# Setup of a cross-attention kernel: Wk loaded in its own row order and turned ahead of y, and four head sums of batch 14 moved to ScalarE and Pool

## The chip, the cores and the metric

The kernel runs on one core of a Trainium2 chip. The metric is device time in microseconds of one execution, as the median of repeated runs. Beside it one execution was profiled. Engines are called as the profile calls them: PE (TensorE matmul), PEld (its weight loads), DVE (VectorE), ACT (ScalarE), POOL (GpSimd) and SP (SyncE, which here only issues DMAs).

## What is computed

The reference is a cross-attention layer in float32 for 16 batches of 100 queries (640 wide), 718 context rows (384 wide) and 4 extra tokens, with 8 heads of 80:

```
query = x @ Wq;  keyt = enc @ Wk;  valt = enc @ Wv
hs = mha(query, keyt, valt)
ca_q1 = einsum('btc,th->bch', ca, Wq_ca)[:, indices, :]
ca_hs1 = mha(ca_q1, x, x)
ca_hs2 = mha(ca_hs1 @ Wq, ca @ Wk_ca, ca @ Wv_ca)
out = (hs + ca_hs2) @ Wout + b_out + x
```

`mha` is softmax attention over 8 heads. The first line of the second path is small, but its scores go over 100 rows of x per batch.

## The kernel before

**Stages.** A setup part (lines 265 to 1482) loads the weights and makes what all batches share; a loop over 16 batches (line 1494 on) follows, in which every batch makes its scores (`s_ps`, L800), the maximum over keys on DVE, exponentials on ACT, the values' product with the weights (`a_ps`, L1799), and meanwhile the keys (`k_ps`, L481) and values (`v_ps`, L450) of later work. The setup is ordered by a scheduler from the program's text and its data waits, except where a line is bound with `in_order` (kept in program order on its engine) or `tc.issue_after` (after a named instruction). In the batch loop the order on each engine is that of the text (`manual_schedule`).

**Keys by sums.** The products `enc @ Wk` and `enc @ Wv` are made by a scheme with fewer block products (`K_PLAN`, `V_PLAN`): a block product takes a "form", a sum of blocks of `enc`, and a form of the weight, a sum of blocks of Wk. `weight_sums` (L546) makes the weight's forms in place in `wk_sb`: 12 subtractions of 128x256 on DVE. `enc_sums` (L516) makes those of `enc` on POOL. `Keys.go` (L481 for the matmuls, L421 and L423 for their evacuation) takes the forms one after the other, into the PSUM tiles `k_psA` to `k_psE`.

**The weight Wk.** The host hands Wk transposed (`wkt`, 640 rows of heads by 384). The kernel needs it untransposed, with the heads' first 64 columns sorted in `wk_sb` and their last 16 in `wk4`. Before, `load_packed` (L317) does the sorting in the load: eight DMAs of 64 rows and one of the rest, into the room of `kT`. Five groups of three 128x128 transposes on PE (`w_ps`, L1415) follow, and one ACT copy (L1418) for each group.

**y.** `Second.products` (L970) makes `y_ps` = x times `m2`, where `m2` is masked on POOL (`keys`, L941) from `m_sb`; `m_sb` is copied on DVE (L1399) from `m_ps` (L1391), the product of the transposed Wq with the token keys. `take` (L983) copies the first-path numbers `g` out of `y_ps`, for seven heads and then for the eighth; `copy` (L987) takes the rest. `scores1` (L999, L1006) makes the first-path scores `e` on POOL from `g`; `softmax1` (L891 to L1025) takes their maximum off on DVE.

**Wq.** Five loads `wq_in` into `st` (L323) are spread by heads into `wq_sb` on DVE: three copies for each load (L1426 twice, L1432), before `weight_sums`. The queries (`q_ps`, L560) need them.

**PSUM.** Three pools of two buffers each: `ps2` (two banks each), `psk` and `ps1` (one bank each). A tile waits until the last reader of its buffer is done.

**SP's queue.** All its loads stand in one order; a load's semaphore is shared with the load eight places ahead, whose landing it waits for.

**Batch 14.** `read(g)` (L1747, L1759) divides four heads of `a_ps` by their sums and adds the second path's `hs2`: a reciprocal and four DVE instructions. In batch 15, `vv.go` and `top.go` say in which order value products and steps of the maximum stand.

Of the kernel before, what the change touches and what calls it, by code (L numbers as in the profile page):

```python
# [10 lines left out]
ALU = mybir.AluOpType  # L11
# [3 lines left out]
B, S, H = 16, 100, 640  # L15
NH, D = 8, 80
CAD, T = 384, 4
SK = 722 - T
P = 128
HC = H // P  # L20
CC = CAD // P
# [7 lines left out]
ROWS = NH * S  # L29
# [26 lines left out]
for h in range(NH):  # L56
    lo = h * D
    while lo < (h + 1) * D:
        c = lo // P
# [8 lines left out]
RG = 4  # L68


KH = [(0, 64), (64, KN)]


def load_packed(load, to, w):

    rows = w.rearrange("(h k) n -> h k n", h=NH)
    for h in range(NH):
        r, c = divmod(h, RG)
        load(out=to[64 * r : 64 * r + 64, c], in_=rows[h, :64])
    load(out=to[:, 4], in_=rows[:, 64:])  # L80

V_PLAN = [
# [45 lines left out]
def kernel(  # L143
# [18 lines left out]
    nc = tc.nc  # L162
# [14 lines left out]
    def pair(name):  # L177
        tile = ps2.tile([P, 2, 512], F32, tag="ps2", name=name)
        return tile
# [80 lines left out]
    def in_order(dma):  # L260
        tc.keep_in_program_order(dma)
# [5 lines left out]
    wk_sb = const.tile([P, NF, 2, P], F32, name="wk_sb")  # L267
    wk4 = const.tile([P, CC, P], F32, name="wk4")
# [44 lines left out]
    in_order(nc.sync.dma_start(out=xT, in_=xt[0:2].rearrange("b p c s -> p b c s")))  # L313
    ca_0 = small.tile([S, T, S], F32, tag="ca", name="ca_0")
    in_order(nc.sync.dma_start(out=ca_0, in_=cas[0].unsqueeze(0).to_broadcast([S, T, S])))
    load_packed(
        lambda **ends: in_order(nc.sync.dma_start(**ends)), wkt_sb[:, :, :CAD], wkt  # L317
    )
    halves = [t[:, u] for t in sts for u in range(2)]
    room = halves.pop()  # L320
    wq_in = [t[:, :H] for t in halves]
    for c in range(HC):
        in_order(nc.sync.dma_start(out=wq_in[c], in_=wq[c * P : (c + 1) * P]))  # L323
    in_order(nc.sync.dma_start(out=wvca_sb, in_=wvca.rearrange("(c p) n -> p c n", p=P)))
# [199 lines left out]
    def weight_sums(engine, w, late=None, there={}):  # L524


        at = lambda f: there.get(f, w[:, W_AT[f]])
        raw = lambda c, g: w[:, 2 * (c - 1) + g - 1]
        if w is wk4:
            at, raw = w4_form, w4  # L530
        for f, left, right in (
            (0, raw(1, 2), raw(1, 1)),
            (11, raw(2, 2), raw(3, 2)),
            (12, raw(3, 2), raw(3, 1)),
            (5, raw(2, 2), raw(1, 2)),
            (7, raw(3, 2), at(5)),
            (13, raw(3, 1), at(7)),
            (1, raw(2, 1), raw(3, 1)),
            (3, raw(1, 1), at(7)),
            (6, raw(2, 1), raw(1, 1)),  # L540
            (10, raw(3, 1), raw(2, 2)),
            (2, raw(1, 1), raw(2, 2)),
            (14, raw(2, 1), raw(2, 2)),
        ):
            if late is None or late == (f in (5, 7, 13, 3, 14)):
                made = engine.tensor_tensor(at(f), left, right, ALU.subtract)  # L546
        return made
# [401 lines left out]
    class Second:  # L949
# [35 lines left out]
        def copy(self):  # L985
            self.y = y_sbs[self.b % 2]
            nc.scalar.copy(self.y[:, :, :HT], self.y_v[:, :, T:])  # L987
            if self.b > 1:
                self.take(0, NH)
# [398 lines left out]
    for c in range(HC):  # L1388
        m_ps = psum(f"m_ps_{c}")
        for n, heads in enumerate(HEADS):  # L1390
            nc.tensor.matmul(  # L1391
                m_ps[:, heads[0] * B * T : (heads[-1] + 1) * B * T],
                wqt_sb[:, n, c * P : (c + 1) * P],
                k2T[n],
                start=(n == 0),
                stop=(n == HC - 1),
                skip_group_check=True,
            )
        copied = nc.vector.tensor_copy(  # L1399
            m_sb[c].rearrange("p (b h t) -> p h b t", h=NH, t=T),  # L1400
            m_ps.rearrange("p (h b t) -> p h b t", h=NH, b=B),
        )
        nc.sync.dma_start(out=m_d[c], in_=m_sb[c])
    second = Second(0, xT, ca_0)
    enc_sums(enc)
    masked = keys(load_m(0))
    second.products()
    summed = second.take(0, NH - 1)
    second.copy()

    order = (HC - 1, *range(HC - 1))
    for c in order:
        w_ps = psum(f"w_ps_{c}")
        for cc in range(CC):
            nc.tensor.transpose(  # L1415
                w_ps[:, cc * P : (cc + 1) * P], wkt_sb[:, c, cc * P : (cc + 1) * P], ident
            )
        act(  # L1418
            wk_sb[:, c % 2 : 6 : 2, c // 2] if c < HC - 1 else wk4,
            w_ps[:, : CC * P].rearrange("p (a n) -> p a n", a=CC),  # L1420
        )

    with tc.issue_after(summed.ins):
        for c in range(HC):
            for r in range(2):
                nc.vector.tensor_copy(  # L1426
                    wq_sb[:, c, : 4 * P].rearrange("p (n r k) -> p n r k", n=RG, r=2)[
                        :, :, r
                    ],
                    wq_in[c].rearrange("p (r n k) -> p r n k", r=2, n=RG)[:, r, :, :64],  # L1430
                )
            moved = nc.vector.tensor_copy(  # L1432
                wq_sb[:, c, 4 * P :].rearrange("p (h k) -> p h k", h=NH),
                wq_in[c].rearrange("p (h k) -> p h k", h=NH)[:, :, 64:],
            )
    with tc.issue_after(moved.ins):
        made = weight_sums(nc.vector, wk_sb)
    with tc.issue_after(made.ins):
        second.take(NH - 1, NH)
    made = second.scores1()  # L1440
    with tc.issue_after(made.ins):
        weight_sums(nc.gpsimd, wk4)
        nc.scalar.copy(
            sts[0].rearrange("p a r -> p (a r)")[96:],
            low[96:].to_broadcast([P - 96, 2 * ROWS]),
        )
    with tc.issue_after(masked.ins):
        keys(load_m(1))
    last_keys(0, enc)
    first_keys = Keys(0, enc)  # L1450
    first_keys.go(8)
    va = wide("va")[:, : H // 2]
    va_ps = bank("va_ps")
    turn[0] += 1
    for c in range(CC):
        for n in range(2):
            nc.tensor.matmul(
                va_ps[n * B * T : (n + 1) * B * T, : H // 2],
                cat_sb[:, c, :],
                wvca_sb[:, c, n * (H // 2) : (n + 1) * (H // 2)],  # L1460
                start=(c == 0),
                stop=(c == CC - 1),
            )
    nc.scalar.copy(va, va_ps[:, : H // 2])
    va_d = dram.tile([B * T, H], F32, name="va_d")
    for n in range(2):
# [2 lines left out]
            in_=va[n * B * T : (n + 1) * B * T],  # L1469
        )  # L1470
    first_keys.go(NF)
    with tc.issue_after(first_keys.added.ins):
        second.softmax1()

# [18 lines left out]
    for b in range(B):  # L1493
# [59 lines left out]
            kk = Keys(b + 1, enc)  # L1553

        if b == 0:
            second.scores1()
            m_next = load_m(b + 2)
            kk.go(3)
            top.go(3)
# [115 lines left out]
        else:  # L1675
# [67 lines left out]
        def read(g):  # L1743

            a_v = a_vs[g]
            rs = small.tile([S, 4], F32, tag="rs", name=f"rs_{b}_{g}")
            nc.vector.reciprocal(rs.unsqueeze(2), a_v[:, :, D : D + 1])  # L1747
            cols = slice(4 * g * D, 4 * (g + 1) * D)
            if b == 0:
                nc.vector.tensor_tensor(  # L1750
                    hs[:S, cols].rearrange("p (h d) -> p h d", h=4),
                    a_v[:, :, :D],
                    rs.unsqueeze(2).to_broadcast([S, 4, D]),
                    ALU.mult,
                )
# [12 lines left out]
        if b in MIXED:  # L1768
            steps = (0, 6), (0, 18), (1, 6)
# [112 lines left out]
```

## Time and profile before

| | |
|---|---|
| median of 3 runs | 909.16 us (908.6 to 909.4) |
| the profiled execution's own time | 908.96 us |
| its span, first to last instruction | 907.2 us |
| PE busy | 900.4 us, 12200 matmul instructions |
| DVE, POOL, ACT busy | 719.7, 705.8, 460.1 us |
| granted TensorE clock | 1.000 |

A row of a timeline gives the start, the length, the engine and line, the operation, out<-in and shapes, a count, and in brackets how long the engine was idle before and what ended that. Rows of matmuls are merged and overlap, since a matmul's record runs on while the next has begun; the step from one row's start to the next row's start is what the engine spent.

### The profile page before, as it was taken

The numbers are of one execution on the slowest core, as the hardware profiler recorded it, in microseconds if no ns is written. First come the engines' busy times: TensorE is split into PE (matmuls) and PEld (weight loads), VectorE is DVE, ScalarE is ACT, GpSimd is POOL, SyncE is SP. The second block draws the span as 40 slices with busy tenths as digits, with TensorE's granted clock in tenths as the row PEclk, the third lists the DMA queues.
The fourth block names the chain that finished last, engine by engine and source line by source line (L and its number), as shares of the span: only waits on it lengthen the run. The fifth ranks groups of instructions, "written<-read, shape, count | busy, mean of one in ns | idle before, by whom it ended". The sixth has DMA issues, their size and how long they took to land.

```text
span 907.2 us, 28486 instructions
## 1 busy us (share of the span) xinstructions
PE 900.4 (99%) x12200; PEld 747.1 (82%) x12200; DVE 719.7 (79%) x1285; ACT 460.1 (51%) x906; POOL 705.8 (78%) x683
## 2 busy tenths in 40 slices
PE   9999999999999999999999999999999999999998
PEld 6798889787797878878798787988879788797866
DVE  3569796989849898796987969888984899849983
ACT  2345543747437573644737446374742747436441
POOL 7687999797868879696896959958797688967623
PEclk9999999999999999999999999999999999999999
DMA  8731103031301312130121301103130031300211
GB/s 265 262 120 57 48 14 87 24 107 53 112 4 44 88 33 74 54 105 32 48 60 54 106 33 53 56 25 106 54 83 32 24 107 53 98 32 25 60 44 40
DMA packets 50730, 62.99 MB, mean 69 GB/s; under 512 B 13698, under 2 KB 37954, under 8 KB 50604
## 3 DMA queue, kind: packets, MB, share of 16 engines
q1 hardware_dynamic: 48956, 59.18, 21.4%
q8 instruction: 96, 1.57, 0.7%
q10 hardware_dynamic: 1024, 1.15, 0.4%
q0 software_dynamic: 624, 0.85, 0.3%
q14 instruction: 30, 0.25, 0.1%
HBM read 55.59 MB, written 5.57 MB: 67 GB/s over the span
## 4 chain that ended last, share of the span: by engine, by line
PE 92%; DVE 4%; DMA 2%; SPq 1%; issue 0%; ACTq 0%; DVEq 0%
PE a_ps L1799 12%; PE s_ps L800 11%; PE v_psA L450 10%; PE k_psA L481 9%; PE v_psB L450 8%; PE k_psB L481 7%; PE o_ps L1278 5%; PE k_psA L761 4%; PE v_psC L450 3%; PE k_psC L481 3%; PE q_ps L618 2%; PE q_ps L560 2%; PE v_psD L450 2%; PE v_psE L450 2%; PE q_psA L618 1%; DMA xT<-in_xt 1%
## 5 line engine op out<-in xcount | busy, mean ns | idle before, releaser
L999 POOL TENSOR_TENSOR e<-ca,g 100x800 f32<-100x800 f32 x64 | 100.7, 1584 | 98.6 <-ACT kT L423 78.7
L1799 PEld LDWEIGHTS a_ps<-vs,st 120*64 120x64 f32 (+3 forms) x3072 | 119.0, 124 | 10.1 <-issue 0.7
L1799 PE MATMUL a_ps<-vs,st 120*64 120x81 f32 (+3 forms) x3072 | 122.8, 233 | 0.0
L516 POOL TENSOR_TENSOR enc<-enc 128x240 f32<-128x240 f32 x144 | 109.1, 768 | 11.3 <-DMA enc<-in_enct 4.2
L1515 DVE TENSOR_TENSOR st<-st,over 120x1600 f32<-120x1600 f32 x48 | 115.1, 2400 | 0.0
L450 PE MATMUL v_psA<-wv_sb,enc 128*120 128x320 f32 x352 | 109.3, 433 | 0.0
L1110 POOL TENSOR_TENSOR hs<-vb,p 100x640 f32<-100x640 f32 x64 | 93.1, 1466 | 9.6 <-issue 4.8
L1117 POOL TENSOR_TENSOR hs<-hs,hs 100x640 f32<-100x640 f32 x48 | 93.2, 1942 | 3.8
L481 PE MATMUL k_psA<-enc,wk_sb 128*128 128x240 f32 x384 | 95.4, 371 | 0.6 <-DVE wk_sb L546 0.6
L1006 POOL TENSOR_TENSOR e<-e,e 100x800 f32<-100x800 f32 x48 | 91.9, 1914 | 3.8
L450 PE MATMUL v_psB<-wv_sb,enc 128*120 128x320 f32 x296 | 91.9, 433 | 0.0
L1523 ACT ACTIVATE st<-st 120x1600 f32<-120x1600 f32 x48 | 73.9, 1539 | 25.1 <-DVE st L1515 24.7
L481 PEld LDWEIGHTS k_psA<-enc,wk_sb 128*128 128x128 f32 x384 | 71.4, 190 | 17.1 <-DVE wk_sb L546 1.0
L450 PEld LDWEIGHTS v_psA<-wv_sb,enc 128*120 128x120 f32 x352 | 64.2, 183 | 25.0 <-DVE vs L421 0.5
L1527 DVE TENSOR_TENSOR most<-most,st 120x800 f32<-120x800 f32 x64 | 67.0, 1047 | 13.8 <-ACT st L850 12.3
L481 PE MATMUL k_psB<-enc,wk_sb 128*128 128x240 f32 x320 | 77.9, 366 | 0.0
L800 PE MATMUL s_ps<-qp,kT 64*56 64x100 f32 (+1 forms) x3072 | 73.7, 248 | 0.3 <-issue 0.3
L800 PEld LDWEIGHTS s_ps<-qp,kT 64*56 64x56 f32 (+1 forms) x3072 | 67.2, 130 | 5.9 <-issue 4.6
L450 PEld LDWEIGHTS v_psB<-wv_sb,enc 128*120 128x120 f32 x296 | 54.1, 183 | 21.9 <-DVE vs L421 0.4
L856 ACT COPY st<-s_ps 120x800 f32<-120x800 f32 x64 | 49.8, 830 | 39.6 <-PE s_ps L800 39.4
L1185 ACT COPY hsT<-turned_hs 32x160 f32<-32x160 f32 (+7 forms) x244 | 67.7, 278 | 3.0
L481 PEld LDWEIGHTS k_psB<-enc,wk_sb 128*128 128x128 f32 x320 | 60.7, 190 | 8.1
(209 smaller groups left out, 1898.3 us busy)
## 6 DMA issues: line engine op xcount, KB each, us to landing
vb<-va_d SPq DMA_DIRECT2D x62, 250.0 KB
enc<-in_enct SPq DMA_DIRECT2D x30, 240.0 KB
enc<-in_enct SPq DMA_DIRECT2D x15, 360.0 KB
xT<-in_xt SPq DMA_DIRECT2D x8, 500.0 KB
rest<-in_enct SPq DMA_DIRECT2D x31, 120.0 KB
xn<-in_x SPq DMA_DIRECT2D x11, 320.0 KB
out<-xn SPq DMA_DIRECT2D x11, 320.0 KB
ca<-in_cas SPq DMA_DIRECT2D x16, 156.2 KB
```

What stands on the lines that cost most here:

```text
L450: nc.tensor.matmul(at[0][j][:KN, : H // 2], a_form(self.enc, f)[:, j * KN : (j + 1) * KN], wv_there.get(f, wv_sb[:, W_AT[f]]), start=first ...
L481: nc.tensor.matmul(at[:, i * KT : (i + 1) * KT], wk_sb[:, W_AT[f], i], a_form(self.enc, f), start=(first and i == 0), stop=last, skip_grou ...
L516: nc.gpsimd.tensor_tensor(out, left, right, op)
L800: nc.tensor.matmul(s_ps[at][k0:k1, cols], w, rhs, start=not begun & {(at, k) for k in range(k0, k1, 32)}, stop=last, skip_group_check=True,)
L999: first = nc.gpsimd.tensor_tensor(to, self.ca[:, t, :].unsqueeze(1).to_broadcast([S, NH, S]), g[:, :, t].unsqueeze(2).to_broadcast([S, NH, ...
L1006: made = nc.gpsimd.tensor_tensor(e, e, to, ALU.add)
L1110: first = nc.gpsimd.tensor_tensor(to, self.vb[t][:S].rearrange("p (h d) -> p h d", h=NH), p2[:, :, t].unsqueeze(2).to_broadcast([S, NH, D] ...
L1117: nc.gpsimd.tensor_tensor(sums, sums, to, ALU.add)
L1185: nc.scalar.copy(self.hsT(r)[32 * m : 32 * m + 32, :, first - lo : end - lo], turned[32 * i : 32 * i + 32, :, m, first - at : end - at],)
L1515: return nc.vector.tensor_tensor(st[i], st[i], top.over[:KN].unsqueeze(1).to_broadcast([KN, 2, ROWS]), ALU.subtract,)
L1523: nc.scalar.activation(st[i], st[i], AF.Exp, scale=SCALE)
L1799: nc.tensor.matmul(a_v[lo:hi, h % 4], st[i // 2][: KEYS[i], i % 2, h * S + lo : h * S + hi], block(i, h // 4)[: KEYS[i], h % 4], start=(i ...
```

## The change

1. **Load of Wk.** Nine sorted loads become two in the weight's own row order (row blocks 0 and 1, then 2 to 4), and they stand ahead of the loads of x (`xT`) and of the tokens (`ca`), no longer behind them.
2. **Transposes.** `turn_wk(cc)` turns one of three column blocks in five transposes into a two-bank tile of `ps2`. The heads are sorted by its copies: ACT takes `wk4` (128 elements) and one half of `wk_sb` (256), DVE the other half (256). Blocks 0 and 1 stand ahead of y, block 2 behind it.
3. **Wq.** `weight_sums` comes first; then DVE spreads three of the five loads, and ACT the other two, behind the first eight steps of the keys.
4. **Smaller moves.** The fill of 32 rows of `sts[0]` (`st<-low`, ACT) stands behind the first keys. In batch 0 the first-path scores of batch 1 wait for the running maximum (`seen`). The first matmul for `va` is kept in program order.
5. **Batches 14 and 15.** The four products of the first half of batch 14 go to ACT, and one POOL addition of 100x320 adds `hs2`. In batch 15 the third of the value steps comes ahead of the last step of the maximum.

```
-    load_packed(
-        lambda **ends: in_order(nc.sync.dma_start(**ends)), wkt_sb[:, :, :CAD], wkt
-    )
+    for c0, c1 in ((0, 2), (2, HC)):
+        in_order(
+            nc.sync.dma_start(
+                out=wkt_sb[:, c0:c1, :CAD],
+                in_=wkt[c0 * P : c1 * P].rearrange("(c p) n -> p c n", p=P),
+            )
+        )
+    in_order(nc.sync.dma_start(out=xT, in_=xt[0:2].rearrange("b p c s -> p b c s")))
+    in_order(nc.sync.dma_start(out=ca_0, in_=cas[0].unsqueeze(0).to_broadcast([S, T, S])))
...
+    def turn_wk(cc):
+        w_ps = pair(f"w_ps_{cc}").rearrange("p a n -> p (a n)")
+        for c in range(HC):
+            made = nc.tensor.transpose(
+                w_ps[:, c * P : (c + 1) * P], wkt_sb[:, c, cc * P : (cc + 1) * P], ident
+            )
+            if c == 0:
+                in_order(made)
+        act(
+            wk4[:, cc].rearrange("p (h k) -> p h k", h=NH),
+            w_ps[:, :H].rearrange("p (h k) -> p h k", h=NH)[:, :, 64:],
+        )
+        for g, copy in enumerate((act, dve)):
+            copy(
+                wk_sb[:, 2 * cc + g].rearrange("p i (r k) -> p i r k", r=2),
+                w_ps[:, :H].rearrange("p (r i g k) -> p g i r k", r=2, i=2, g=2)[
+                    :, g, :, :, :64
+                ],
+            )
...
+    turn_wk(0)
+    turn_wk(1)
     second = Second(0, xT, ca_0)
     enc_sums(enc)
     masked = keys(load_m(0))
     second.products()
-    summed = second.take(0, NH - 1)
+    second.take(0, NH - 1)
     second.copy()
...
+    turn_wk(2)
+    made = weight_sums(nc.vector, wk_sb)
...
+    with tc.issue_after(made.ins):
+        moved = spread_wq(dve, range(3))
     with tc.issue_after(moved.ins):
-        made = weight_sums(nc.vector, wk_sb)
-    with tc.issue_after(made.ins):
         second.take(NH - 1, NH)
     made = second.scores1()
...
     first_keys.go(8)
+    spread_wq(lambda *ends: tc.keep_in_program_order(act(*ends)), range(3, HC))
...
-            second.scores1()
+            second.scores1(seen)
...
+            vv.go(3)
+            top.go()
             vv.go(2)
-            top.go()
-            vv.go(3)
...
+                if b == B - 2 and g == 0:
+                    nc.scalar.mul(hs[:S, part], a_v[:, h, :D], rs[:, h : h + 1])
+                    continue
...
+            if b == B - 2 and g == 0:
+                nc.gpsimd.tensor_tensor(hs[:S, cols], hs[:S, cols], hs2[:, cols], ALU.add)
```

**PE, from y to the first keys.** In these rows `y_ps` is y, `w_ps` a group of transposes (its input `kT` is the room that Wk was loaded into), `kT_ps` the keys of the last 128 columns, which need `wk4`. Before:

```order
L970 MATMUL y_ps_358<-m_142,xT_121 36x108
L1415 MATMUL w_ps_372<-ident,kT 128x128 x3
L970 MATMUL y_ps_358<-m_142,xT_121 64x72
L970 MATMUL y_ps_358<-m_142,xT_121 36x72
L1415 MATMUL w_ps_377<-ident,kT 128x128 x3
L1415 MATMUL w_ps_387<-ident,kT 128x128
L1415 MATMUL w_ps_382<-ident,kT 128x128 x3
L1415 MATMUL w_ps_387<-ident,kT 128x128 x2
L702 MATMUL kT_ps_453<-enc_97,wk_88 128x240
L1415 MATMUL w_ps_392<-ident,kT 128x128 x3
L702 MATMUL kT_ps_453<-enc_97,wk_88 128x240 x2
```

Of the change, from the end of y (its last two rows) to the second pass over `k_psA`; the ten transposes of blocks 0 and 1 stand ahead of all ten rows of y:

```order
L951 MATMUL y_ps_369<-m_135,xT_121 64x72
L951 MATMUL y_ps_369<-m_135,xT_121 36x72
L1389 MATMUL w_ps_383<-ident,kT 128x128 x5
L683 MATMUL kT_ps_441<-enc_97,wk_88 128x240 x3
L683 MATMUL kT_ps_441<-rest_98,wk_88 128x240
L683 MATMUL kT_ps_441<-enc_97,wk_88 128x240 x4
L683 MATMUL kT_ps_441<-rest_98,wk_88 128x240
L462 MATMUL k_psA_453<-enc_97,wk_sb 128x240 x2
L462 MATMUL k_psB_457<-enc_97,wk_sb 128x240 x2
L462 MATMUL k_psD_461<-enc_97,wk_sb 128x240 x2
L462 MATMUL k_psA_453<-enc_97,wk_sb 128x240 x2
```

The transposes moved from behind y to ahead of it, all but five, and `k_psD`, which stood ahead of the first `k_psA`, now stands behind `k_psB`.

**DVE, the same stretch.** `wq_sb<-st` is the spread of Wq, `wk_sb<-wk_sb` the subtractions, `g` the copy out of y whose last piece POOL waits for. Before:

```order
L1426 COPY wq_sb<-st_82 128x4x64 x2
L1432 COPY wq_sb<-st_82 128x128
L1426 COPY wq_sb<-st_83 128x4x64 x2
L1432 COPY wq_sb<-st_83 128x128
L546 TENSOR_TENSOR wk_sb<-wk_sb 128x256 x12
L983 COPY g_369<-y_ps_358 100x4
L421 TENSOR_TENSOR kT<-k_psA_465,kT 128x2x240
```

Of the change:

```order
L1399 COPY wk_sb<-w_ps_342 128x256
L964 COPY g_380<-y_ps_369 100x28
L527 TENSOR_TENSOR wk_sb<-wk_sb 128x256 x3
L1399 COPY wk_sb<-w_ps_383 128x256
L527 TENSOR_TENSOR wk_sb<-wk_sb 128x256 x8
L1421 COPY wq_sb<-st_81 128x4x64 x2
L1427 COPY wq_sb<-st_81 128x128
L1421 COPY wq_sb<-st_81 128x4x64 x2
L1427 COPY wq_sb<-st_81 128x128
L1421 COPY wq_sb<-st_82 128x4x64 x2
L1427 COPY wq_sb<-st_82 128x128
L964 COPY g_380<-y_ps_369 100x4
```

The subtractions came ahead of the spread, four of them ahead of the last block's copy; the first `k_psA` product needs the fifth subtraction behind that copy (form 7, in place 5 of `wk_sb`). A copy of DVE out of a `w_ps` waits until ACT's two copies out of it are done.

**SP, the loads behind the first context rows.** Before:

```order
L287 DMA enc_97<-in_enct 128x240 x3
L313 DMA xT_121<-in_xt 128x2x500
L315 DMA ca_123<-in_cas 100x400
L317 DMA kT<-in_wkt 64x384 x8
L317 DMA kT<-in_wkt 128x1x384
L323 DMA st_81<-in_wq 128x640 x2
```

Of the change:

```order
L264 DMA enc_97<-in_enct 128x240 x3
L296 DMA kT<-in_wkt 128x2x384
L296 DMA kT<-in_wkt 128x3x384
L301 DMA xT_121<-in_xt 128x2x500
L302 DMA ca_122<-in_cas 100x400
L304 DMA st_81<-in_wq 128x640 x2
```

Seven loads are gone, and Wk stands where x stood.

More of the change, by code (lines that the diff above doesn't have):

```diff
@@ L71 @@
 KH = [(0, 64), (64, KN)]
[L74 to L80, printed above, removed]
 V_PLAN = [
@@ L312 @@
     xT = inp.tile([P, 2, HC, S], F32, tag="xT", name="xT_0")
-    in_order(nc.sync.dma_start(out=xT, in_=xt[0:2].rearrange("b p c s -> p b c s")))
     ca_0 = small.tile([S, T, S], F32, tag="ca", name="ca_0")
-    in_order(nc.sync.dma_start(out=ca_0, in_=cas[0].unsqueeze(0).to_broadcast([S, T, S])))
-    load_packed(
-        lambda **ends: in_order(nc.sync.dma_start(**ends)), wkt_sb[:, :, :CAD], wkt
-    )
     halves = [t[:, u] for t in sts for u in range(2)]
@@ L1407, with spread_wq @@
     second.products()
-    summed = second.take(0, NH - 1)
+    second.take(0, NH - 1)
     second.copy()
[L1411 to L1424, printed above, removed]
+    turn_wk(2)
+    made = weight_sums(nc.vector, wk_sb)
+    def spread_wq(copy, chunks):
+        for c in chunks:
             for r in range(2):
-                nc.vector.tensor_copy(
+                copy(
                     wq_sb[:, c, : 4 * P].rearrange("p (n r k) -> p n r k", n=RG, r=2)[
@@ L1431 @@
                 )
-            moved = nc.vector.tensor_copy(
+            moved = copy(
                 wq_sb[:, c, 4 * P :].rearrange("p (h k) -> p h k", h=NH),
@@ L1435 @@
             )
+        return moved
+    with tc.issue_after(made.ins):
+        moved = spread_wq(dve, range(3))
     with tc.issue_after(moved.ins):
-        made = weight_sums(nc.vector, wk_sb)
-    with tc.issue_after(made.ins):
         second.take(NH - 1, NH)
@@ L1442 @@
         weight_sums(nc.gpsimd, wk4)
[L1443 to L1446, printed above, removed]
     with tc.issue_after(masked.ins):
@@ L1456 @@
         for n in range(2):
-            nc.tensor.matmul(
+            made = nc.tensor.matmul(
                 va_ps[n * B * T : (n + 1) * B * T, : H // 2],
@@ L1463 @@
             )
+            if c == n == 0:
+                in_order(made)
     nc.scalar.copy(va, va_ps[:, : H // 2])
@@ L1471 @@
     first_keys.go(NF)
+    in_order(
+        nc.scalar.copy(
+            sts[0].rearrange("p a r -> p (a r)")[96:],
+            low[96:].to_broadcast([P - 96, 2 * ROWS]),
+        )
+    )
     with tc.issue_after(first_keys.added.ins):
```

## The prediction

> **What bounds the kernel now.** I read the page first, then the waits of PE, then PE's windows and timeline where those waits lie, then the chain of waits there, and at last the other engines beside it. The page's first line, and the shares by engine of the chain that ended last:
>
> ```profile
> span 907.2 us, 28486 instructions
> PE 92%; DVE 4%; DMA 2%; SPq 1%; issue 0%; ACTq 0%; DVEq 0%
> ```
>
> The span is 907.2 us, and the end is set by PE. So an edit counts only if it takes away PE work or a wait of PE, or adds one. These are PE's three longest waits of the whole run (total, times, longest; none other is over 0.3):
>
> ```profile
> PE idle_ps L1352 <- DVE idle L1349: 1.1, 1, 1.1
> PE k_psA L481 <- DVE wk_sb L546: 0.6, 1, 0.6
> PE w_ps L1415 <- DMA kT<-in_wkt: 0.6, 1, 0.6
> ```
>
> Two of them, 0.6 us each, are what the setup part of the change touches: the first keys wait for a subtraction, and the transposes wait for the load of Wk. Windows of PE (length, then PE busy) tell how much is to be had there, and how little behind it:
>
> ```profile
> 27.30:36.28 8.98, 7.72 (x59) 1.00 1.00 341
> 49.87:907.30 857.43, 853.11 (x11876) 1.00 0.19 58
> ```
>
> From the start of y to the first `k_psA`, PE is idle for 1.26 us of 8.98; its pipeline hides some more. After 49.87 it is busy for 99.5%. The stretch itself, row by row:
>
> ```profile
> 27.31 0.83 PE L970 MATMUL y_ps<-m,xT 128*64 128x72 f32 x16
> 28.76 0.52 PE L1415 MATMUL w_ps<-ident,kT 128*128 128x128 f32 x3 [0.62 <-DMA kT<-in_wkt]
> ...
> 29.48 1.20 PE L1415 MATMUL w_ps<-ident,kT 128*128 128x128 f32 x9
> 30.52 0.57 PE L702 MATMUL kT_ps<-enc,wk 128*128 128x240 f32 x2
> ...
> 32.63 1.78 PE L702 MATMUL kT_ps<-enc,wk 128*128 128x240 f32 x8
> 34.26 0.57 PE L702 MATMUL kT_ps<-rest,wk 128*128 128x240 f32 x2
> 34.66 0.97 PE L481 MATMUL k_psD<-enc,wk_sb 128*128 128x240 f32 x4
> 36.28 1.08 PE L481 MATMUL k_psA<-enc,wk_sb 128*128 128x240 f32 x4 [0.64 <-DVE wk_sb L546]
> ```
>
> What ended last before that last row is in the chain (the start, the length, the piece):
>
> ```profile
> 26.98 5.91 DMA st<-in_wq
> ...
> 33.54 2.69 DVE wk_sb L546 x8
> ```
>
> The fifth load of Wq lands at 32.89, DVE spreads it, and only then subtracts; the eighth subtraction, 2.69 us on, frees `k_psA` at 36.23.
>
> **The gain, if nothing new waits.** Step costs come from dense runs: nine transposes from 29.48 to 30.52, 0.116 us each; eight `kT_ps` products from 32.63 to 34.26, 0.204 each. For y I take these two rows of batch 0:
>
> ```profile
> 65.97 0.96 PE L970 MATMUL y_ps<-m,xT 128*64 128x72 f32 x20
> 66.86 1.08 PE L481 MATMUL k_psA<-enc,wk_sb 128*128 128x240 f32 x4
> ```
>
> They give 0.89 us for all of y. The same work packed from 27.31: 15 transposes 1.73, y 0.89, 18 products `kT_ps` 3.67, together 6.29, so `k_psA` could start at 33.60 where it started at 36.28. That is 2.68 earlier, but the first `k_psD`, 0.81 by the four products of the chain's next row, went ahead of it and now stands behind. **Bound of the gain: 1.87 us.**
>
> ```profile
> 37.35 0.81 PE k_psB L481 x4
> ```
>
> **Loads.** Transposes now stand first at 27.31, so Wk must have landed. SP before:
>
> ```profile
> 10.91 0.52 SPq L313 DMA_DIRECT2D xT<-in_xt  x1
> 11.98 13.04 SPq L317 DMA_DIRECT2D kT<-in_wkt  x9
> ```
>
> By the chain, the load of x issued at 10.91 landed at 23.17. Wk's first load takes that slot and is smaller; I estimate both of Wk by 22 to 24. x and the tokens come behind with no wait of SP for lanes of seven more loads, x near 25 (needed at 28.5), Wq near 26 to 30, needed only behind the subtractions, near 34. All are covered; if Wk's cover of 3 us were gone, each us of it would be a us of PE.
>
> **DVE and ACT, the new chain.** Copies out of the transposes have these neighbours:
>
> ```profile
> 29.32 0.48 ACT L1418 COPY wk<-w_ps 128x384 f32<-128x384 f32 x1 [8.07 <-PE w_ps L1415]
> 29.83 0.37 ACT L987 COPY y_sb<-y_ps 100x256 f32<-100x256 f32 x1
> 27.42 0.69 DVE L1399 COPY m<-m_ps 128x512 f32<-128x512 f32 x1 [0.63 <-PE m_ps L1391]
> 29.60 0.19 DVE L983 COPY g<-y_ps 100x28 f32<-100x28 f32 x1 [1.30 <-PE y_ps L970]
> ```
>
> So ACT takes 0.27 for 128 elements (below 0.37 by the 0.1 that 384 adds over 256) and 0.37 for 256; DVE 0.43 for 256, halfway between its two rows. A subtraction is 0.34 (2.69 over 8). ACT began 0.56 after the first of three transposes; with five it begins at 28.10 and is done with block 0 at 28.74. DVE: its copy of block 0 to 29.21, one subtraction to 29.55, the copy of block 1 to 29.98, `g` to 30.15. PE: ten transposes to 28.47, y to 29.36, block 2 to 29.94; then the first `kT_ps` waits for DVE's copy of block 1, some 0.08. The third `kT_ps` product needs block 2 of `wk4`. ACT has `y_sb` ahead of that copy, and `y_sb` waits for `g`: 30.18 to 30.55, `wk4` to 30.82, where PE is ready at 30.43. **That is a new wait of about 0.4, 0.5 with the 0.08.** `k_psA` then comes at 34.1. Its form is the fifth subtraction behind DVE's copy of block 2: three subtractions to 31.16, the copy behind ACT's last one from 31.22 to 31.65, five subtractions to 33.33. 0.7 us is spare there.
>
> The subtractions get a new neighbour, POOL's masks for batch 1:
>
> ```profile
> 26.25 0.97 POOL L941 TENSOR_TENSOR m<-m,hmask 128x96 f32<-128x96 f32 x3
> 28.87 2.15 POOL L941 TENSOR_TENSOR m<-m,hmask 128x96 f32<-128x96 f32 x4
> 64.85 2.02 DVE L1527 TENSOR_TENSOR most<-most,st 120x800 f32<-120x800 f32 x2 [0.95 <-ACT st L850]
> 67.46 3.23 DVE L1527 TENSOR_TENSOR most<-most,st 120x800 f32<-120x800 f32 x2
> ```
>
> The masks took 0.32 each with DVE on PSUM and 0.54 beside its copies in SBUF; DVE's maximum took 1.01 an instruction alone and 1.61 beside `e` on POOL, which started 0.2 later. So either engine can hold up the other. One subtraction stands ahead of `g` and three behind. Held up for nothing at the least and 0.54 (one mask) at the most, the one ahead adds 0 to 0.54 to PE's wait; I take 0.1, nearer to nothing, since the masks start late in its span. The other three have 0.7 of cover. **Sum: 1.87 - 0.5 - 0.1 = about 1.3 us gained.**
>
> The Trainium skill, "SBUF — State Buffer", section "SBUF: two separate sides", speaks against putting subtractions there: it calls the port pair that VectorE shares with GpSimd an exclusive lock, held for a whole instruction, so that a VectorE operation with two SBUF inputs waits out a GpSimd operation that reads SBUF. By it all four would wait, and the sum would be the first rival's below. The 1.61 against 1.01 agrees with a hold-up, not with one for the whole of POOL's 2.16 us.
>
> **Edits taken at nothing.** Two Wq loads (six copies, at most 0.48 each like the 384-element row) on ACT, and the fill behind the first keys:
>
> ```profile
> 44.13 0.43 ACT L1464 COPY va<-va_ps 128x320 f32<-128x320 f32 x1 [5.37 <-PE va_ps L1457]
> 31.39 1.52 ACT L1443 COPY st<-low 32x1600 f32<-32x1600 f32 x1
> ```
>
> ACT idles 5.37 us there, more than the six copies' 2.9. The fill can hold the first copy of a query back by some 0.4, and PE needs that buffer only four chunks later. Without the cover it would cost up to 1.5. In batch 0 POOL's scores of batch 1 wait for the maximum:
>
> ```profile
> 67.68 4.41 POOL L999 TENSOR_TENSOR e<-ca,g 100x800 f32<-100x800 f32 x2 [3.54 <-ACT st L856]
> 88.92 1.00 DVE L891 STREAM_TRANSPOSE turned<-e 128x800 f32<-128x800 f32 x1
> ```
>
> They would start up to 3 us later. The seven `e` steps need some 13.5 us, to 81.2 before; DVE reads the sum at 88.92, so 7 us cover it. Batch 14:
>
> ```profile
> 856.01 0.35 ACT L753 COPY kT<-k_psA 64x240 f32<-64x240 f32 x1 [2.83 <-PE k_psC L761]
> 873.01 0.24 POOL L1081 TENSOR_TENSOR e<-s,mx 100x32 f32<-100x32 f32 x1 [18.28 <-DVE mx L1079]
> 862.81 0.57 PE L800 MATMUL s_ps<-qp,kT 64*64 64x100 f32 x16 [0.34 <-issue]
> ```
>
> ACT is idle for 2.83 us and POOL for 18.28 where they get work. PE's only gap nearby is 0.34 with no engine named, so DVE's four instructions fewer free nothing that PE waits for. ACT's four products may delay the copy at 856.01; PE has other work between.
>
> **The rivals.** (1) *DVE is held up through the masks.* All four subtractions wait for half to all of a 0.54 mask. The one ahead of `g` puts 0.27 to 0.54 on PE's wait, the other three 0.8 to 1.6 against 0.7 of cover, so 0.1 to 0.9. The gain shrinks to 1.87 - 0.5 - 0.4 to 1.4, around 0.5: 908.4. For it: the two rows above. Against: the masks end near 31. (2) *The time saved is given back*: PE comes 1.3 us earlier to batch 0 and waits there for DVE or POOL, whose work didn't shrink: about 909.1. Against: PE's waits in the batches are a few tenths. (3) *The end gains too*: the 0.34 gap, 0.58 by steps, goes with other instruction streams: about 907.0. The row bears it out weakly, since no engine is named. (4) *Slower: PE stands behind Wk's load.* With transposes ahead of y nothing is left to fill the wait. If Wk lands later than 27.31, PE loses a us for each us; from 28.6 the gain is gone, from 30.4 the kernel is over 0.2% slower, and at 30.8, about 911. For it: the ninth load before landed only at 28.7. Against: that one was issued up to 14 us behind x.
>
> **How the numbers follow.** 0.2%, 1.82 us, is about what a measurement of this kernel can tell from no change; faster means below 907.34. Against the profiled execution's own 908.96, the forecast is 907.66; against the median of 909.16, 907.86. I say **907.7**, with its own range from 907.1 (no new wait) to 908.3. Chances: forecast 0.60; rival 1 0.14; rival 2 0.09; rival 3 0.11; rival 4 0.06. The range, 906.7 to 908.9, takes in rivals 1 and 3 and leaves out the other two. Faster: 0.20 of the forecast's 0.60 and 0.10 of rival 3, so 0.30; slower 0.06; the rest, 0.64, is the same.
>
> **What would show it.** Right: transposes from 27.3 without a wait for the load; `k_psA` near 34.1; a wait of PE at the third `kT_ps` for ACT; subtractions of 0.34 behind the masks. Wrong: a wait of PE for `in_wkt`; a `wk_sb` wait ahead of `k_psA`, with subtractions over 0.6; or `k_psA` early and a new wait in batch 0 or 1.

## The result, and the profile after

| | kernel before | changed kernel |
|---|---|---|
| median, 21 runs each on one chip | 908.36 us (906.73 to 909.72) | 906.35 us (905.47 to 907.87) |
| ratio, 95% interval | | 0.9979 (0.9973 to 0.9986) |
| the profiled execution's own time, its span | 908.96, 907.2 us | 907.72, 906.0 us |

The change makes the kernel 1.9 us faster (1.3 to 2.5, by the interval times 908.36). The forecast was a gain of 1.3 us, at the low edge of that, and a time of 907.7 in a range from 906.7: the measured 906.35 lies below the range. 0.8 us of the miss is the level of the kernel before, which was 909.16 in the three runs that the forecast started from and 908.36 in 21; the rest is a gain that was sized too small.

PE's waits of the whole run in the changed kernel (total, times, longest):

```profile
PE idle_ps L1333 <- DVE idle L1330: 1.1, 1, 1.1
PE k_psC L462 <- DVE vs L402: 0.3, 1, 0.3
PE k_psA L462 <- DVE kT L402: 0.2, 1, 0.2
```

Both waits of the setup that the forecast spoke of, 0.6 us for Wk's load and 0.6 for a subtraction, are gone. A new one stands in the list: 0.2 us at `k_psA` for DVE's sums of the keys. PE's timeline of the changed kernel, from the first transpose to the first query:

```profile
27.31 1.26 PE L1389 MATMUL w_ps<-ident,kT 128*128 128x128 f32 x10
28.50 0.96 PE L951 MATMUL y_ps<-m,xT 128*64 128x72 f32 x20
29.39 0.77 PE L1389 MATMUL w_ps<-ident,kT 128*128 128x128 f32 x5
29.99 1.40 PE L683 MATMUL kT_ps<-enc,wk 128*128 128x240 f32 x6
31.22 0.57 PE L683 MATMUL kT_ps<-rest,wk 128*128 128x240 f32 x2
31.63 1.78 PE L683 MATMUL kT_ps<-enc,wk 128*128 128x240 f32 x8
33.25 0.57 PE L683 MATMUL kT_ps<-rest,wk 128*128 128x240 f32 x2
33.65 0.97 PE L462 MATMUL k_psA<-enc,wk_sb 128*128 128x240 f32 x4
...
47.77 2.53 PE L541 MATMUL q_ps<-xT,wq_sb 128*128 128x200 f32 x14
```

No row carries a bracket: PE runs from 27.31 to 47.77 without a wait. `k_psA` starts at 33.65; packed without any wait, the forecast had it at 33.60. In the windows (length, PE busy) the stretch is full, where it held 1.26 us of idle time before:

```profile
27.30:33.65 6.35, 6.35 (x55) 1.00 0.96 358
33.65:47.77 14.12, 14.12 (x74) 1.00 0.47 139
47.77:906.00 858.23, 853.73 (x11876) 1.00 0.20 59
```

The **setup stretch**, from PE's first instruction at 27.31 to the first query, is 47.77 - 27.31 = 20.46 us. Before, the same stretch ended with this row, and was 49.87 - 27.31 = 22.56:

```profile
49.87 0.33 PE L560 MATMUL q_ps<-xT,wq_sb 128*128 128x200 f32 x1
```

So the setup gained 2.10 us, in one profile against one. The profiled executions differ by only 1.24; 0.6 of the rest is lost at one place in batch 1 (below), and some 0.2 stays open.

On DVE and ACT, the rows that the forecast's chain of copies was built on:

```profile
28.63 0.42 DVE L1399 COPY wk_sb<-w_ps 128x256 f32<-128x256 f32 x1 [0.23 <-ACT wk_sb L1399]
29.09 0.42 DVE L527 TENSOR_TENSOR wk_sb<-wk_sb 128x256 f32<-128x256 f32 x1
29.43 0.42 DVE L1399 COPY wk_sb<-w_ps 128x256 f32<-128x256 f32 x1
29.77 0.18 DVE L964 COPY g<-y_ps 100x28 f32<-100x28 f32 x1
29.88 1.34 DVE L527 TENSOR_TENSOR wk_sb<-wk_sb 128x256 f32<-128x256 f32 x3
31.15 0.41 DVE L1399 COPY wk_sb<-w_ps 128x256 f32<-128x256 f32 x1
31.48 2.76 DVE L527 TENSOR_TENSOR wk_sb<-wk_sb 128x256 f32<-128x256 f32 x8
```

```profile
29.98 0.37 ACT L968 COPY y_sb<-y_ps 100x256 f32<-100x256 f32 x1 [0.83 <-DVE g L964]
30.25 0.27 ACT L1394 COPY wk<-w_ps 128x128 f32<-128x128 f32 x1
30.40 0.39 ACT L1399 COPY wk_sb<-w_ps 128x256 f32<-128x256 f32 x1
```

`g` ended at 29.95 (forecast 30.15) and the last block of `wk4` at 30.52 (forecast 30.82). The three subtractions beside POOL's masks took 0.42 each from start to start (29.88 to 31.15), the eight behind them 0.34.

### The profile page after: what moved, and what is told of

It reads as the page before. It is cut to its first block, busy times and chain, and to the rows that moved or that the text cites. A ratio compares the mean times of both kernels' runs of the same rounds, so it can differ in the third digit from the quotient of the medians.

```text
span 906.0 us, 28486 instructions
## 1 busy us (share of the span) xinstructions
PE 900.3 (99%) x12200; PEld 748.1 (83%) x12200; DVE 720.6 (80%) x1278; ACT 461.9 (51%) x917; POOL 712.8 (79%) x684
## 4 chain that ended last, share of the span: by engine, by line
PE 94%; DVE 5%; ACT 0%; DMA 0%; issue 0%; DVEq 0%
PE a_ps L1806 12%; PE s_ps L781 12%; PE v_psA L431 10%; PE k_psA L462 8%; PE v_psB L431 8%; PE k_psB L462 6%; PE o_ps L1259 5%; PE k_psA L742 4%; PE v_psC L431 3%; PE k_psC L462 3%; PE v_ps L372 2%; PE q_ps L599 2%; PE q_ps L541 2%; PE v_psD L431 2%; PE v_psE L431 2%; PE k_psE L462 1%
## 5 line engine op out<-in xcount | busy, mean ns | idle before, releaser
L980 POOL TENSOR_TENSOR e<-ca,g 100x800 f32<-100x800 f32 x64 | 97.9, 1540 | 90.9 <-ACT kT L404 67.4
L497 POOL TENSOR_TENSOR enc<-enc 128x240 f32<-128x240 f32 x144 | 113.2, 796 | 14.2 <-DMA enc<-in_enct 7.2
L1091 POOL TENSOR_TENSOR hs<-vb,p 100x640 f32<-100x640 f32 x64 | 90.6, 1426 | 3.8 <-DMA vb<-va_d 1.5
```

Source lines behind the costliest of these rows:

```text
L497: nc.gpsimd.tensor_tensor(out, left, right, op)
L980: first = nc.gpsimd.tensor_tensor(to, self.ca[:, t, :].unsqueeze(1).to_broadcast([S, NH, S]), g[:, :, t].unsqueeze(2).to_broadcast([S, NH, ...
L1091: first = nc.gpsimd.tensor_tensor(to, self.vb[t][:S].rearrange("p (h d) -> p h d", h=NH), p2[:, :, t].unsqueeze(2).to_broadcast([S, NH, D] ...
```

## The experiments

Each kernel is the kernel before or the changed kernel with one edit. They ran in three groups, each on one chip with the kernel before beside it: the four of the first heading; the first three of the second with the first run of the kernel "kept apart"; and the others. The kernel before had 908.36, 908.14 and 908.41 us there. A ratio is to the kernel before of the same group; ratios and intervals stand as the measurement gave them, and differ by up to 0.0007 from the quotient of the two medians. Beside the time, the setup stretch is given, since it is free of what happens later.

### Each part alone

**Setup only.** The changed kernel with its edits to batches 14 and 15 taken back: `read(0)` of batch 14 on DVE again, and `vv.go(2)`, `top.go()`, `vv.go(3)` in the order of before.

> The change without its edits to batches 14 and 15. Theory (the setup carries the whole gain: PE's two waits around y and the keys): the time of the full change, 906.35 us, about 2.0 under the kernel before; in the profile k_psA starts at 33.65 as in the full change. Rival (the end gains too, since the gap of 0.5 us before the last scores is gone in the full change): 906.9, a gap of about 0.5 at that place.

906.86 us, ratio 0.9980 (0.9971 to 0.9989); stretch 20.46. The gap ahead of the last scores was not there either (in before, it was the row at 862.81 with 0.34 idle):

```profile
858.24 3.01 PE L781 MATMUL s_ps<-qp,kT 64*64 64x100 f32 x128
```

The setup carries most of the gain, and the gap doesn't belong to the edits of batch 14. The time alone doesn't settle it: 906.86 is the rival's figure, 0.9980 is nearly the ratio of the full change (0.9979), and the interval holds both 906.35 and 906.9.

**Batches 14 and 15 only**, the same edits made to the kernel before.

> The kernel before with only the edits to batches 14 and 15. Theory (PE waits for none of these instructions): no change, a ratio of 1.0000 within 0.0005. Rival (the end gains): 0.5 us faster, ratio 0.9994, and no gap before the last scores.

908.40 us, ratio 0.9993 (0.9983 to 1.0002): no difference from the kernel before, though the interval holds the rival's 0.5 us too. No row before the last scores shows idle time, as the rival said, but neither does one in the kernel with only Wk's loads moved (below), which lacks these edits. What tells more is that this kernel has the setup of before, instruction for instruction, and yet its profile differs there from the profile of before:

```profile
31.95 0.50 DVE L1426 COPY wq_sb<-st 128x256 f32<-128x256 f32 x2
32.37 0.22 DVE L1432 COPY wq_sb<-st 128x128 f32<-128x128 f32 x1
32.50 4.11 DVE L546 TENSOR_TENSOR wk_sb<-wk_sb 128x256 f32<-128x256 f32 x12
```

The spread of the fifth load of Wq began at 31.95 where it began at 32.91 in before, the subtractions with it, and the stretch was 48.89 - 27.18 = 21.71 instead of 22.56. PE's wait for Wk's load isn't in this profile at all. So **the old setup varies with its loads**, by 0.85 us in two draws, and against this draw the new setup gains only 21.71 - 20.46 = 1.25 us. The new one gave 20.45 or 20.46 in all seven profiles of kernels with its setup order (the others follow below).

**The subtractions ahead of the spread of Wq**, alone, in the kernel before:

```
     with tc.issue_after(summed.ins):
+        made = weight_sums(nc.vector, wk_sb)
+    with tc.issue_after(made.ins):
         for c in range(HC):
...
     with tc.issue_after(moved.ins):
-        made = weight_sums(nc.vector, wk_sb)
-    with tc.issue_after(made.ins):
         second.take(NH - 1, NH)
```

> The kernel before with one edit: the twelve subtractions stand ahead of the spread of Wq on DVE. Theory (the first keys waited for Wq's fifth load and its spread through DVE's order): the wait of 0.81 and the slow restart of 0.26 go, k_psA starts at 34.66 right behind kT_ps, the wait for Wk's load (0.87) stays: 1.1 us faster, ratio 0.9988. Rival (the last transposes' copies on ACT are the next to be late): k_psA at 35 or later, under 0.7 us gained.

```profile
27.74 0.83 PE L970 MATMUL y_ps<-m,xT 128*64 128x72 f32 x16
28.96 0.52 PE L1415 MATMUL w_ps<-ident,kT 128*128 128x128 f32 x3 [0.39 <-DMA kT<-in_wkt]
...
34.45 0.57 PE L702 MATMUL kT_ps<-rest,wk 128*128 128x240 f32 x2
34.85 0.97 PE L481 MATMUL k_psA<-enc,wk_sb 128*128 128x240 f32 x4
```

The mechanism is as expected: `k_psA` behind `kT_ps` without a wait, the wait for Wk still there, and the stretch 21.78, 0.78 under before. The time is not: 908.09 us, ratio 0.9997 (0.9988 to 1.0005), 0.3 us where 1.1 was expected. 0.3 of that went at 40, where the fill of `st`, now behind the keys' first copies on ACT, held one of them up, a sum on DVE waited for it, and PE for the sum; 0.7 went in batch 1 (2.63 us instead of 1.89 from `v_psA` to `k_psE`, as under "The loss in batch 1").

**Wk's nine loads ahead of those of x and the tokens**, alone, in the kernel before:

```
-    in_order(nc.sync.dma_start(out=xT, in_=xt[0:2].rearrange("b p c s -> p b c s")))
-    ca_0 = small.tile([S, T, S], F32, tag="ca", name="ca_0")
-    in_order(nc.sync.dma_start(out=ca_0, in_=cas[0].unsqueeze(0).to_broadcast([S, T, S])))
     load_packed(
         lambda **ends: in_order(nc.sync.dma_start(**ends)), wkt_sb[:, :, :CAD], wkt
     )
+    in_order(nc.sync.dma_start(out=xT, in_=xt[0:2].rearrange("b p c s -> p b c s")))
+    ca_0 = small.tile([S, T, S], F32, tag="ca", name="ca_0")
+    in_order(nc.sync.dma_start(out=ca_0, in_=cas[0].unsqueeze(0).to_broadcast([S, T, S])))
```

> The kernel before with one edit: Wk's nine loads stand ahead of those of x and the tokens. Theory (two waits in a row on PE, of which only the later one counts): the transposes no longer wait for their load, but the first keys still wait for Wq's fifth load and its spread, so k_psA stays near 36.3 and the time too, ratio 1.0000 within 0.0007; if x now lands behind 27.3, y waits, and that is hidden as well up to 1.8 us. Rival (each wait counts for itself): 0.9 us faster, ratio 0.9990.

```profile
PE k_psA L481 <- DVE wk_sb L546: 1.2, 1, 1.2
PE k_psD L481 <- DVE wk_sb L546: 0.2, 1, 0.2
```

The wait for Wk is gone from the list, and the wait for the subtraction has grown from 0.6 to 1.2: `k_psA` started at 36.40, where it was 36.28. Nothing was gained; 909.43 us, ratio 1.0015 (1.0002 to 1.0028). The two waits stood one behind the other, and only the later one counted. The stretch was 49.97 - 27.11 = 22.86. That the time came out slower was not expected: DVE waited 1.04 us for the fifth load of Wq, and the runs reached from 907.1 to 912.7:

```profile
33.03 0.50 DVE L1426 COPY wq_sb<-st 128x256 f32<-128x256 f32 x2 [1.04 <-DMA st<-in_wq]
```

### The changed kernel with one edit undone

**Three loads of Wq spread on DVE ahead of the subtractions** (`spread_wq(dve, range(3))` bound behind `take(0, NH - 1)`, `weight_sums` behind it).

> The change with one edit: DVE spreads its three loads of Wq ahead of the subtractions again (nine copies, about 1.6 us, behind the first copy out of y). Theory (place of the subtractions in DVE's order is half of the gain): the ninth subtraction, which the first k_psA product needs, ends near 35.0 where PE is ready at 33.65, so PE waits 1.3 and restarts slowly (0.26): 1.6 us slower than the change, 907.9, ratio to the kernel before 0.9996. Rival (the room in front of the keys is larger than read): 906.4, no wait at k_psA.

```profile
31.81 4.10 DVE L527 TENSOR_TENSOR wk_sb<-wk_sb 128x256 f32<-128x256 f32 x12
```

906.82 us, ratio 0.9983 (0.9974 to 0.9992), stretch 20.94. `k_psA` waited 0.24 and started at 33.95; the sixth of these twelve ends at 31.81 + 6 x 0.34 = 33.85. So here the first `k_psA` product needs the sixth subtraction, and not the ninth, on which the expected loss of 1.6 stood; the stretch lost 0.48. This doesn't carry over to the changed kernel, since the edit also changed the order of the subtractions. The product takes form 7 in both. `weight_sums` writes form 7 over a block of Wk that forms 11 and 12 still read, so it comes behind these two. In this kernel the scheduler issues the forms 0, 11, 12, 5, 1 and then 7, the sixth. In the changed kernel it issues 0, 5, 6 and 2 ahead of the last copy and 1, 11, 12, 10 and then 7 behind it, the ninth, as the section on the change has it. There form 7 is ready at 31.48 + 5 x 0.34 = 33.18, a little over 0.4 us before PE comes at 33.65.

**Wk's two loads behind x and the tokens.**

> The change with one edit: Wk's two loads stand behind those of x and the tokens. Theory (two loads instead of nine, not their place, take the wait away; Wk landed at 20.5 in the change and may land 2 us later): no wait at the transposes, 906.35, ratio 0.9979. Rival (the place matters, as the forecast took it): a wait of PE for in_wkt near 27.3 and up to 1 us more.

906.63 us, ratio 0.9983 (0.9974 to 0.9991), stretch 20.46, no wait for a load. Two loads in place of nine are enough; the place in the queue isn't needed. The 20.5 of the expectation is early for Wk as a whole: in the changed kernel SP waited 1.1 us for one of Wk's loads and issued the load of `wvca`, which stands eight places behind Wk's second one, at 22.16.

```profile
SPq L305 <- DMA kT<-in_wkt: 1.1, 1, 1.1
```

**All transposes behind y.**

> The change with one edit: all fifteen transposes stand behind y. Theory (the transposes ahead of y fill PE's wait for POOL's last masks, and start the chain of copies early): y waits about 0.6 for the mask that ends at 28.6, the copies out of the transposes come about 1.5 later, k_psA near 34.9 instead of 33.65: 1.3 us slower than the change, 907.6, ratio 0.9993. Rival (DVE and ACT have room): 906.4 to 906.9.

```profile
PE w_ps L1389 <- DVE wk_sb L1399: 0.5, 1, 0.5
PE y_ps L951 <- POOL m L922: 0.4, 1, 0.4
```

907.77 us, ratio 0.9999 (0.9990 to 1.0007); the stretch is 22.00, 1.5 longer than in the change. As expected, y waits for POOL's mask. The copies out of the transposes come later too, but PE meets them at the last five transposes and not at `k_psA`, where the expectation had it. So this order is worth most of the gain. The profile is of the slowest of the twelve runs (909.77), in which PE reached the stretch only at 29.00; the stretch is counted from there.

**`seen` taken out**: in batch 0, POOL's scores of batch 1 wait for nothing.

> The change with one edit undone: in batch 0 POOL's scores of batch 1 no longer wait for the running maximum. Theory (DVE's two steps of the maximum run beside POOL and take 1.6 instead of 1.0 us each, but PE has room there): within 0.2 us of the unedited change. Rival (the wait is part of the gain): 0.6 us or more above it, with a new wait of PE on DVE before 100 us.

906.76 us, ratio 0.9985 (0.9977 to 0.9994), stretch 20.45; the change unedited had 906.49 and 0.9982 (0.9973 to 0.9990) beside it (next heading). No difference that these runs can tell, and no new wait of PE on DVE before 100 us.

### The loss in batch 1

In batch 1 of the changed kernel, DVE and then POOL:

```profile
110.53 0.19 DVE L1060 TENSOR_REDUCE mx<-s 100x8 f32<-100x32 f32 x1
110.83 1.28 DVE L1062 TENSOR_TENSOR e<-s,mx 100x32 f32<-100x32 f32 x1
112.03 0.81 DVE L402 TENSOR_TENSOR vs<-v_psA,vs 120x640 f32<-120x640 f32 x1
```

```profile
110.52 3.03 POOL L980 TENSOR_TENSOR e<-ca,g 100x800 f32<-100x800 f32 x2
```

A subtraction of 100x32 took 1.28 us. POOL's first score had begun 0.31 before it and ended near 112.04 (half of 3.03), where DVE's ended at 112.11. In the kernel before, the same subtraction took 0.44, since POOL began its score only behind it:

```profile
112.85 0.44 DVE L1081 TENSOR_TENSOR e<-s,mx 100x32 f32<-100x32 f32 x1
113.97 3.03 POOL L999 TENSOR_TENSOR e<-ca,g 100x800 f32<-100x800 f32 x2
```

So it is in all fourteen profiles of this document: the subtraction took 1.26 to 1.29 us in the eight where POOL's score began before it, and 0.43 to 0.45 in the six where it began behind. When it is held up, DVE's sums of the keys come late, and PE waits. The Trainium skill, "SBUF — State Buffer", section "SBUF: two separate sides", calls the ports that VectorE shares with GpSimd an exclusive lock for a whole instruction, when a VectorE operation with two SBUF inputs meets a GpSimd operation that reads SBUF; the 1.28 us agree with it. The subtractions beside POOL's masks in the setup don't show it: they took 0.08 us more, where one of these masks took 0.32 in the kernel before with DVE on PSUM.

**The two kept apart**: in batch 1, POOL's first score waits for that subtraction instead of the running maximum.

```
-            second.scores1(seen, range(T - 1))
+            if b > 1:
+                second.scores1(seen, range(T - 1))
...
-            now.scores2(nc.vector if b == 1 else nc.gpsimd)
+            less = now.scores2(nc.vector if b == 1 else nc.gpsimd)
+            if b == 1:
+                second.scores1(less, range(T - 1))
```

> The change with one edit: in batch 1, POOL's first-path scores of batch 2 wait for DVE's small subtraction (e<-s,mx, 100x32) instead of for the running maximum. In the change's profile that subtraction took 1.28 us instead of 0.44, as long as POOL's first score was running beside it, and PE then lost 0.6 us at the keys at 114 to 116. Theory (DVE waits out POOL's instruction, and PE waits for DVE): the subtraction takes 0.44 again, PE loses nothing there, 0.5 us faster than the change, 905.8, ratio 0.9973. Rival (DVE is late there for another reason): the loss of 0.6 us stays, 906.4.

906.26 us, ratio 0.9977 (0.9969 to 0.9986). It ran a second time, beside the change unedited:

> The change itself, unedited, beside the next three on one chip. Theory: ratio to the kernel before 0.9979 as in its own runs, 906.4 us; in the profile the stretch from the first transpose to the first query is 20.46 us again, and the keys at 114 to 116 lose 0.6 again, if POOL's first score runs beside DVE's small subtraction.

> The change with the small subtraction of batch 1 kept apart from POOL's first score, as in e9_apart. Theory (the 0.6 us lost at the keys of batch 1 are kept): 0.4 to 0.6 us under the unedited change of the same call, near 905.9. Rival (given back later in the batches): within 0.2 us of the unedited change.

The change again: 906.49 us, ratio 0.9982 (0.9973 to 0.9990), stretch 20.46. Kept apart: 906.34 us, 0.9979 (0.9970 to 0.9988). PE at the keys of batch 1, first in the change again, then kept apart:

```profile
112.83 1.24 PE L431 MATMUL v_psA<-wv_sb,enc 128*120 128x320 f32 x4
114.27 1.05 PE L462 MATMUL k_psA<-enc,wk_sb 128*128 128x240 f32 x4 [0.20 <-DVE kT L402]
115.34 0.88 PE L462 MATMUL k_psE<-enc,wk_sb 128*128 128x240 f32 x3
```

```profile
113.22 1.24 PE L431 MATMUL v_psA<-wv_sb,enc 128*120 128x320 f32 x4
114.30 0.97 PE L462 MATMUL k_psA<-enc,wk_sb 128*128 128x240 f32 x4
115.11 0.97 PE L462 MATMUL k_psE<-enc,wk_sb 128*128 128x240 f32 x4
```

From `v_psA` to `k_psE` it is 2.51 us in the one and 1.89 in the other: the loss of 0.6 us is DVE's hold-up, and it goes when that goes (the subtraction took 0.44 again). In the time only 0.15 us of it can be seen, as the rival had it (within 0.2), and that is within the intervals. In these two profiles the 0.6 isn't given back: from the first query to the end it is 905.4 - 47.56 = 857.8 us in the change and 904.9 - 47.95 = 857.0 kept apart. But this part scatters too: 856.9 to 858.2 in the eight profiles with the hold-up, 856.3 to 857.4 in the six without. Why the medians show so little stays open. This version is the fastest of those that ran, but not by more than the measurement can tell.

### The third product of kT_ps

The changed kernel with the copy of `g` made twelve times, and the copies of y and of `wk4` bound behind it:

```
-    second.take(0, NH - 1)
-    second.copy()
-    turn_wk(2)
-    made = weight_sums(nc.vector, wk_sb)
+    for _ in range(12):
+        taken = second.take(0, NH - 1)
+        in_order(taken)
+    with tc.issue_after(taken.ins):
+        second.copy()
+        turn_wk(2)
+        made = weight_sums(nc.vector, wk_sb)
```

> The change with the copy of g out of y made twelve times on DVE (0.11 us each), and the copies of y and of the last block of wk4 bound behind it on ACT: it moves the copy that the third kT_ps product needs from 30.5 to about 31.4. Theory (each product is two records of 0.204, so the third starts at 30.8 and the copy was 0.3 early): PE waits 0.6 for ACT inside kT_ps. Rival (the forecast's reading, in which the third product was ready at 30.4): PE waits 1.0.

```profile
29.98 0.98 PE L683 MATMUL kT_ps<-enc,wk 128*128 128x240 f32 x4
32.81 0.67 PE L683 MATMUL kT_ps<-enc,wk 128*128 128x240 f32 x2 [1.85 <-ACT wk L1396]
```

907.85 us in one run. The twelve copies took 2.62 us, twice what I had reckoned, so the sizes of both expectations are off; the place is not. Four records run, and the fifth waits for ACT's copy of `wk4`. That copy ended at 32.75 here and at 30.52 in the change, 2.23 later; PE waited from 30.79, when it was ready, to 32.81, which is 2.02. The difference, 0.2 us, is the room that the change has at this place. There is no wait, but little more would make one.

## Why the forecast was right and wrong

- **What bounds the kernel** was right: two waits of PE in the setup, one behind the other. Alone, the load order gained nothing, and the subtractions first gained 0.78 us of stretch, of which 0.3 could be seen in the time; the order of the transposes, the loads and the subtractions together gave 2.10 us of stretch.
- **The bound of the gain, 1.87 us, was too small by 0.23.** Up to the first `k_psA` it held: 36.28 - 33.65 - 0.81 = 1.82 was gained, 0.05 less than packed. But behind that, to the first query, the old order took 49.87 - 36.28 = 13.59 and the new one 47.77 - 33.65 - 0.81 = 13.31 (`k_psD`, 0.81, stands there now). The 0.28 between them are three records of before that follow a wait and step by 0.31, 0.31 and 0.28 to the next, where others step by 0.20: at 36.28 behind DVE, and at 38.00 and 46.55 behind ACT's copies out of `k_psA`, for which the weight loads of these products waited:

```profile
38.00 0.70 PEld L481 LDWEIGHTS k_psA<-enc,wk_sb 128*128 128x128 f32 x4 [0.21 <-ACT kT L423]
46.52 0.50 PEld L481 LDWEIGHTS k_psA<-enc,wk_sb 128*128 128x128 f32 x3 [0.18 <-ACT kT L423]
```

In the change `k_psD` stands between the two passes, and none of the three is slow. So 1.82 + 0.28 = 2.10, by the profile of before from which the forecast was made.
- **The step that failed: the new wait of 0.5 us at the third `kT_ps` product.** I took 0.204 us as the time of a product and put the third one at 30.43. A product of this kind shows as two records in the profile: the order lists nine products where the timeline counts 18 records, and both stood in front of me. The third product starts with the fifth record, at 30.8. The right count alone, in the forecast's own sum, gives 29.94 + 0.08 + 4 x 0.204 = 30.84 against `wk4` at 30.82, and the wait is gone. The 0.08 ahead of the first product isn't there either: it starts at 29.99 without a wait. And the chain was shorter: ACT's copy of 128 elements cost 0.15 from start to start, not 0.27, and DVE's copy of 256 out of PSUM 0.34, not 0.43. The wait does not exist, with 0.2 us to spare. Without the 0.5 for it, the 0.1 for the masks, and with the 0.23 above, the forecast's sum is the 2.10 that the stretch gained.
- **The room in front of `k_psA`** was read rightly as that of the fifth subtraction behind the last copy: ready at 33.2, forecast 33.33. The room was 0.4 us, not 0.7, because PE came at 33.65 and not at 34.1. This changed nothing in the sum.
- **Rival 1, DVE held up through the masks:** the three subtractions took 0.42 instead of 0.34, in all 0.24 us, and had room. The forecast's 0.1 for the one ahead of `g` was too much: its copy followed 0.34 behind it.
- **Rival 2, time given back later,** happened in part, at 114 to 116, for 0.6 us. But not for the reason given: in the kernel with only Wk's loads moved, PE reached the first query at 49.97, later than before, and lost 0.5 there. It is decided by whether POOL's score begins before or behind DVE's small subtraction.
- **Rival 3, the gap of 0.34 at 862,** was also missing in the profile without the edits to batch 14, and there in the one with the subtractions first. It comes and goes; the edits to batches 14 and 15 gave no gain that the runs can tell.
- **Rival 4, Wk late,** never came near: with the loads behind x and the tokens there was still no wait. The estimate of 22 to 24 for its landing was close: SP's wait for it in the changed kernel ended at 22.16.
- **The level.** The forecast took the median of three runs for the kernel before. Its runs reach from 906.5 to 910.9 in all groups, those of the change from 905.5 to 907.9; in the 21 runs of each on one chip it is 3.0 us against 2.4. The old order hung on the landing of Wq's fifth load, and the new one does not; the two profiles of the old setup show that this moves the time, but not how much of the scatter it makes. Both kernels scatter ahead of the stretch as well: PE reached it between 27.10 and 27.74 in thirteen of the fourteen profiles. It took the level and the mis-sized gain together to fall below the range: 907.7 less the 0.8 of the level, or less the 0.8 by which the stretch gained more than 1.3, is 906.9, which lies inside. What the profiles don't explain is that the medians differ by 1.9 to 2.0 us, where the two profiled executions differ by 1.24.

## What to carry to other kernels

Before pricing a wait in a chain, count what one record of the profile stands for: set the count of a row beside the count of instructions in the order. Where two waits stand one behind the other on the engine that sets the end, taking away the earlier one alone bought nothing here, and taking away the later one alone bought 0.78 us of stretch out of 2.10; the sum of an edit holds only if both go. A load that a chain hangs on can move the time from run to run; take more than three runs as the level to forecast from. An edit to a part that a scheduler orders can change more than it says: read the order again before carrying a result from one kernel to another.

## What was not expected of the hardware

- A DVE subtraction of 100x32 took 1.28 us instead of 0.44 beside a POOL instruction of 1.5 that had started 0.3 earlier, while subtractions of 128x256 beside POOL's masks took only 0.08 more each.
- Behind a wait, PE's first record of the keys steps by 0.31 us instead of 0.20 (36.28 to 36.58 in the kernel before), so that a wait cost about 0.1 more than its idle time.
- Copies of 28 elements on DVE, twelve times into the same tile, took 0.22 us each, where a single one let the next, another instruction start after 0.11.
